# Issuing some of a megakernel's stores and small transfers from ScalarE's DMA queue in place of SyncE's

## The chip, the core and the metric

One core of one Trainium2 chip runs the whole program in one launch. The metric is the device time of an execution in microseconds (us), as the median of several runs. The engines are TensorE (PE, matrix products; PEld its weight loads), VectorE (DVE), ScalarE (ACT, activations and copies), GpSimd (POOL) and SyncE (SP), which in the kernel before only issues DMAs. Each engine runs its own list of instructions in order, and semaphores join the lists.

## The reference

Two layers act on x of 2 x 512 x 512 in float32. Each layer is an attention part and a feed-forward part, and a row of adaptive shifts, scales and gates (from `c` and `wmod`) stands around both.

```python
h = layernorm(x) * (1 + ca) + sa
x = x + ga * L0_attn(h)     # gated linear attention: 32 heads of 128, 8 key heads, chunks of 128
h = layernorm(x) * (1 + cb) + sb
x = x + gb * L0_ffn(h)      # product with a weight of signs, a scale and a bias
...                         # the second layer's own c and wmod
x = x + ga * L1_attn(h)     # softmax attention: 32 heads of 16, 8 key heads, rope, biases
h = layernorm(x) * (1 + cb) + sb
x = x + gb * L1_ffn(h)      # four streams mixed by a 4 x 4 matrix after 50 Sinkhorn iterations
```

What the change touches is the second layer's attention: `softmax(q k^T / 4) v` for each of 32 heads of 16 over 512 tokens, where four query heads share a key and value head.

## The kernel before, in words

**Layer 0** is cut into 64 units of one key head's group of four query heads, one batch and one chunk of 128 tokens. A loop over the units writes the code of each: `scores` (line 523) loads a row of decays `gb` by DMA (L530), masks it on POOL (`dec`, L532), exponentiates it on ACT (L79) and multiplies it with the scores on DVE (L545); `state`, `mix`, `turn` and `project_out` follow. Weights come in by `raw_tile` (L220), are split into a high half on ACT (L229) and a low half on POOL (L232), and each float32 product is made of three products of halves (L254). The halves of an activation are made alike: the high one on ACT (`exact`, L490), the low one on DVE (L491).

**Between the layers**, `tail` (L726) runs beside the later units: the last norms and the feed-forward part of layer 0, and, for each batch, the projections of layer 1. `project_kv` (L717) makes keys and values, `project_q` (L721) one of four tiles of queries. `rope_halves` (L700) takes a projection, adds the bias on ACT (L697), rotates it on DVE and POOL (L704 to L707), copies the result to its high half `hi` on ACT (L709), subtracts that on POOL for the low half `lo` (L711), and stores both in DRAM (L713). `project_kv` stores the values (L719). All these stores are issued from SP's queue.

**Layer 1's attention** has 16 steps (`order`): a batch, a half of the queries and one of four tiles of heads. `queries1` (L849) and `keys1` (L834) load the halves from DRAM into tiles `qs` and `ks`, where the rows of `qs` are high half, low half, high half for each of two head groups, 96 rows in all, and rows 96 to 99 stay free. A step has eight pieces. `maxima_` multiplies queries with keys on PE (L899) and takes each row's maximum over 512 keys on DVE (L903). After every fourth piece the maxima are split into halves (L913 on ACT, L914 on POOL), turned by PE (L917), copied by ACT to a tile `mm` of eight rows and 256 columns (L922), and sent by DMA into rows 96 to 99 of `qs` (L923). There `weigh_` uses them: its product with 100 rows (L937) gives the scores less their maximum, which ACT exponentiates straight out of PSUM (`pt`, L79). `outputs` multiplies the result with the values on PE (`op`, L957) and copies it to `os` on ACT (L971); `finish_` turns it (L980), divides on DVE (L984, L986) and adds it to x on POOL (L992). Ten pieces lie between the maxima of a piece and its weighing (`LAG`).

**Layer 1's streams** follow each half batch: the norm, 50 Sinkhorn iterations on DVE and POOL (L1191 to L1211) and the mix on PE (L1258). The last ones end the program.

**The order of the work.** The code is written in one order of units and pieces, and a scheduler then arranges every engine's list with a model of the instructions' times, priorities (`tc.high_priority`) and added order edges. Such edges are kept in `anchor`: the last instruction of a kind on an engine, behind which the work of `behind()` and `gated()` is kept on the same engine. `scores` sets `anchor["sp"]` to its load of `gb` (L530), and `maxima_` sets it to the transfer of L923. SP's queue holds every DMA of the program, 639 of them, in one order: a DMA whose source or buffer is not ready holds up those behind it. [...]

The DMAs that the change concerns are `k_dram<-hi` and `q_dram<-hi` (L713, 2 and 8 times), `v_dram<-raw` (L719, 2) and `qs<-mm` (L923, 32).

Of the kernel before, what the change touches and what calls it, by code (L numbers as in the profile page):

```python
# [9 lines left out]
FP = mybir.dt.float32  # L10
# [33 lines left out]
H1, KV1, D1 = 32, 8, 16  # L44
# [9 lines left out]
def tile_adaln(ctx: ExitStack, tc: tile.TileContext, a: dict, out: bass.AP):  # L54
    nc = tc.nc
# [82 lines left out]
    anchor = {}  # L138
# [33 lines left out]
    def temp(shape, dt, name, bufs=2):  # L172
        return wk.tile(shape, dt, name=name, bufs=bufs)
# [205 lines left out]
    for kc in range(KC):  # L379
# [13 lines left out]
        out=upto, in_=all1, pattern=[[1, P]], compare_op=ALU.is_ge, fill=0.0, base=0, channel_multiplier=-1,  # L393
# [73 lines left out]
    def project(n, hh, b):  # L467
        hi, lo = W[n, hh]
        ps = bank([P, L], "pps")
        passes(ps, [((hi[:, kc * P:(kc + 1) * P], lo[:, kc * P:(kc + 1) * P]), hcol(b, kc)) for kc in range(KC)])  # L470
        return ps
# [223 lines left out]
    def biased(n, t, i, b):  # L695
        raw = temp([P, L], FP, "raw1")
        nc.scalar.activation(raw, project(n, t, b), AF.Identity, bias=l1c["bias"][:, i:i + 1])  # L697
        return raw

    def rope_halves(n, t, i, b, dst):  # L700

        raw = biased(n, t, i, b)
        rot = temp([P, L], FP, "rot1")
        nc.vector.stream_shuffle(rot, raw, [j ^ 8 for j in range(32)])  # L704
        nc.gpsimd.tensor_tensor(raw, raw, l1c["rope"][0], ALU.mult)
        nc.vector.tensor_tensor(rot, rot, l1c["rope"][1], ALU.mult)
        (nc.gpsimd if RA else nc.vector).tensor_tensor(raw, raw, rot, ALU.add)  # L707
        hi = temp([P, L], FR, "hi1")
        nc.scalar.copy(hi, raw)  # L709
        lo = temp([P, L], FR, "lo1")  # L710
        nc.gpsimd.tensor_tensor(lo, raw, hi.bitcast(FP), ALU.subtract)  # L711
        for src, r in ((hi, 0), (lo, D1)):
            nc.sync.dma_start(out=dst[:, r:r + D1, :], in_=src.bitcast(FP))  # L713

    v_dram = [dram.tile([P, L], FP, name=f"v_dram{b}") for b in range(B)]

    def project_kv(b):  # L717
        rope_halves("wk1", 0, 4, b, k_dram[b])
        nc.sync.dma_start(out=v_dram[b], in_=biased("wv1", 0, 5, b))  # L719

    def project_q(b, t):  # L721
        rope_halves("wq1", t, t, b, q_dram[b][8 * t:8 * t + 8])
# [3 lines left out]
    def tail(n):  # L726
# [4 lines left out]
        for b in range(B):  # L731
# [25 lines left out]
            if c == 8:  # L757
                l1c["there", b] = True
                project_kv(b)
                project_q(b, 0)  # L760
                project_q(b, 1)
            elif c in (10, 12):
                project_q(b, c // 2 - 3)
# [54 lines left out]
    def key_tile(i):  # L818
        return i % 2 if i < TWO else (i - TWO + 2) % 3
# [58 lines left out]
    def maxima(st, k):  # L878
        with urgent(st):
            maxima_(st, k)  # L880
# [9 lines left out]
    def maxima_(st, k):  # L890

        assert holder[key_tile(st["i"])] == st["i"]
        rp, j = divmod(k, 4)
        s, i = divmod(j, 2)
        if j == 0:
            st["m"] = small.tile([P, NQ * 2, 2], FP, name="m")
        for qt in range(NQ):
            ps = psp.tile([P, L], FP, name="s1", bufs=S1)
            anchor["pe"] = nc.tensor.matmul(  # L899
                ps, lhsT=st["qs"][rp][0:KS, i, qt * P:(qt + 1) * P], rhs=st["ks"][s][0:KS],  # L900
                start=True, stop=True,
            ).ins
            anchor["dve"] = nc.vector.tensor_reduce(  # L903
                st["m"][:, 2 * qt + s, i:i + 1], ps, AX.X, ALU.max, negate=True
            ).ins
        if j == 3:
            m2 = small.tile([P, NQ * 2, 2, 2], FR, name="m2")
            hi, lo = m2[:, :, 0], m2[:, :, 1]
            if st is order[-1]:
                nc.vector.tensor_copy(hi, st["m"])  # L910
                nc.vector.tensor_tensor(lo, st["m"], hi.bitcast(FP), ALU.subtract)
            else:
                nc.scalar.copy(hi, st["m"])  # L913
                nc.gpsimd.tensor_tensor(lo, st["m"], hi.bitcast(FP), ALU.subtract)  # L914
            mt = psp.tile([8, Q], FP, name="mt", bufs=MT)
            for qt in range(NQ):
                nc.tensor.transpose(  # L917
                    mt[:, qt * P:(qt + 1) * P],
                    m2[:, 2 * qt:2 * qt + 2].bitcast(FP).rearrange("p a b c -> p (a b c)"), ident,
                )  # L920
            mm = temp([8, L], FR, "mm")[:, 0:Q]
            nc.scalar.copy(mm, mt)  # L922
            anchor["sp"] = nc.sync.dma_start(out=st["qs"][rp].bitcast(FP)[96:100], in_=mm.bitcast(FP)).ins  # L923

    def weigh_(st, k):

# [534 lines left out]
    for n, u in enumerate(units):  # L1461
        g, b, c = u["at"]
# [128 lines left out]
```

## Time and profile before

| | |
|---|---|
| median of 3 runs | 1349.3 us (1343.13 to 1351.8) |
| the profiled execution's own time | 1342.29 us |
| its span, first to last instruction | 1340.5 us |
| granted TensorE clock, mean over the span | 0.969 |
| instructions | 23011 |
| DMA | 109.68 MB, mean 82 GB/s |
| ACT busy, 1060 to 1220 us | 125.18 us of 160 |
| PE busy, 1060 to 1220 us | 156.37 us of 160 |

How to read it: the profile is of one execution. Busy time is the time in which an engine's instruction runs; the issue of a DMA, a wait and a branch do not count as busy, and stand under the engine's sequencer (SPq, ACTq). A matmul's end is modelled, so a busy PE is not a PE at its peak. In a line of the timeline stand start, length, engine, line, operation, output and input, and in brackets the idle time before it with what ended it. In a line of waits stand who waited, at which line, for what, and then the total in us, the times, and the longest. A wait for several semaphores is put down to the one that came last by the profile. In a line of stretches stand the stretch, its length, the busy time of PE, PEld, DVE, ACT and POOL with their instructions, the granted clock, the DMA engines' busy share and GB/s. Times from the span's start say where something lies: layer 0's units fill most of the span, the stores of layer 1's first batch begin at about 818 us, those of the second at about 1049 us, and the last transfer of maxima is issued at 1212.9 us.

### The profile page before, as it was taken

To read this page: it belongs to the slowest core of one execution; us is meant where nothing else is said; L and a number is where in the kernel's file an instruction comes from. 1 tells how busy PE (TensorE), PEld (TensorE's weight loads), DVE (VectorE), ACT (ScalarE), POOL (GpSimd) and SP (SyncE) were. 2 spreads that over 40 slices of the span, in tenths; PEclk is the share of its full clock that TensorE was granted. 3 is DMA by queue.
4 is the path that set the end of the run, shared out by engine and by line. 5 is a ranking of instruction groups with operands and counts; after the bars stand their busy time and mean duration, and the time that the engine had idled before them with its cause. 6 is when DMAs were issued, how large, how long until landed. Compare 5 with 4: busy or idle time off the path is not lost. (4 is left out here: it accounts for less than half of the span.)

```text
span 1340.5 us, 23011 instructions
## 1 busy us (share of the span) xinstructions
PE 1227.8 (92%) x7216; PEld 990.3 (74%) x7216; DVE 1090.6 (81%) x2665; ACT 842.1 (63%) x2375; POOL 790.9 (59%) x1233
## 2 busy tenths in 40 slices
PE   6999999999999999999989999898999999995508
PEld 3787887888788788888877788676777777764408
DVE  7888678777686687877989887877879889898888
ACT  4666665476466466766657675665758678775417
POOL 4446564364265367676788888535435856668751
PEclk9999999999999999999999999998999999998659
DMA  8013331231132143332343233424214221200001
GB/s 258 27 35 110 110 95 40 71 104 55 53 99 85 55 151 94 93 97 95 103 127 110 67 123 89 125 85 129 83 30 124 76 75 50 66 16 2 9 8 48
DMA packets 69762, 109.68 MB, mean 82 GB/s; under 512 B 13436, under 2 KB 20348, under 8 KB 69640
## 3 DMA queue, kind: packets, MB, share of 16 engines
q1 hardware_dynamic: 69640, 108.21, 26.6%
q8 instruction: 57, 0.93, 0.3%
q14 instruction: 65, 0.53, 0.1%
HBM read 99.89 MB, written 8.02 MB: 80 GB/s over the span
## 5 line engine op out<-in xcount | busy, mean ns | idle before, releaser
L903 DVE TENSOR_REDUCE m<-s 128x1 f32<-128x512 f32 x256 | 165.7, 670 | 12.4 <-PE s L899 11.8
L79 ACT ACTIVATE pt<-s 128x512 f32<-128x512 f32 x256 | 137.8, 601 | 12.2 <-PE s L937 11.2
L484 POOL TENSOR_TENSOR q<-xcos,rot 128x512 f32<-128x512 f32 x64 | 95.7, 1495 | 36.6 <-DVE xcos L482 32.9
L79 ACT ACTIVATE sg<-sg 128x512 f32<-128x512 f32 x128 | 80.9, 632 | 55.5 <-DVE sg L515 53.6
L899 PE MATMUL s<-ks,qs 96*128 96x512 f32 x256 | 103.7, 433 | 9.3 <-DVE m L903 7.5
L79 ACT ACTIVATE dec<-dec,room 128x128 f32<-128x128 f32 x256 | 82.9, 398 | 43.2 <-POOL dec L532 43.0
L254 PE MATMUL pps<-hh,wq_h 128*128 128x512 f32 x256 | 102.2, 399 | 0.8 <-DVE zl L608 0.8
L532 POOL TENSOR_SCALAR_AFFINE_SELECT dec<-gb 128x512 f32<-128x512 f32 x64 | 47.0, 734 | 93.3 <-DMA gb<-g_dram 46.0
L254 PE MATMUL ops<-wo_h,zl 128*128 128x512 f32 x256 | 100.9, 394 | 1.0 <-DVE zl L608 0.9
L254 PE MATMUL ops<-wo_h,zh 128*128 128x512 f32 x256 | 101.2, 396 | 0.7 <-DVE zl L608 0.7
L254 PE MATMUL gps<-wg_h,hh 128*128 128x512 f32 x256 | 101.0, 395 | 0.7 <-DVE st L574 0.7
L937 PE MATMUL s<-qs,ks 100*128 100x256 f32 x512 | 98.8, 299 | 1.9 <-ACT pt L79 1.4
L254 PE MATMUL gps<-wg_l,hh 128*128 128x512 f32 x256 | 100.5, 393 | 0.0
L254 PE MATMUL pps<-hl,wq_h 128*128 128x512 f32 x256 | 100.3, 392 | 0.0
L254 PE MATMUL pps<-hh,wq_l 128*128 128x512 f32 x256 | 100.2, 391 | 0.0
L254 PE MATMUL ops<-wo_l,zh 128*128 128x512 f32 x256 | 100.1, 391 | 0.0
L254 PE MATMUL gps<-wg_h,hl 128*128 128x512 f32 x256 | 100.1, 391 | 0.0
L595 DVE SCALAR_TENSOR_TENSOR z<-yps,ss,sg 128x128 f32<-128x128 f32 x256 | 71.8, 340 | 31.1 <-ACT ss L79 30.7
L552 POOL TENSOR_TENSOR gb<-gb,q 128x512 f32<-128x512 f32 x48 | 63.8, 1331 | 55.6 <-ACT gb L79 46.4
L585 PE MATMUL yps<-v,dec 128*128 128x128 f32 x512 | 93.0, 277 | 3.1 <-DVE xcos L482 2.8
L937 PEld LDWEIGHTS s<-qs,ks 100*128 100x128 f32 x512 | 82.2, 193 | 18.2 <-ACT pt L79 5.4
L559 POOL TENSOR_TENSOR xw<-v,room 128x512 f32<-128x512 f32 x48 | 57.2, 1205 | 64.7 <-ACT v L499 61.8
(331 smaller groups left out, 3901.7 us busy)
## 6 DMA issues: line engine op xcount, KB each, us to landing
gb<-g_dram SPq DMA_DIRECT2D x64, 256.0 KB
raw<-in_wq SPq DMA_DIRECT2D x56, 256.0 KB
raw<-in_wg SPq DMA_DIRECT2D x48, 256.0 KB
raw<-in_wo SPq DMA_DIRECT2D x48, 256.0 KB
raw<-in_wmod SPq DMA_DIRECT2D x40, 256.0 KB
qs<-q_dram SPq DMA_DIRECT2D x64, 64.0 KB
raw<-in_wk SPq DMA_DIRECT2D x14, 256.0 KB
raw<-in_wv SPq DMA_DIRECT2D x14, 256.0 KB
```

What stands on the lines that cost most here:

```text
L79: ins = nc.scalar.activation(o, i, func, **kw)
L254: nc.tensor.matmul(ps, lhsT=l, rhs=r, start=i == 0, stop=i == n - 1)
L484: nc.gpsimd.tensor_tensor(dst, sp(xc_), sp(rot), ALU.add)
L532: anchor["pool"] = nc.gpsimd.affine_select(out=dec, in_=gb, pattern=[[0, REP0], [1, P]], compare_op=ALU.is_ge, fill=-1e30, base=0, channel ...
L552: nc.gpsimd.tensor_tensor(gb, gb, q[:, c], ALU.mult)
L559: nc.gpsimd.tensor_tensor(xw, u["v"][:, c, :].unsqueeze(1).to_broadcast(sh4), wdc[:, c, r0:r0 + REP0].unsqueeze(2).to_broadcast(sh4), ALU. ...
L585: nc.tensor.matmul(yps[:, h, :], lhsT=u["pr"][:, h, :], rhs=u["v"][:, c, :], start=True, stop=not c)
L595: nc.vector.scalar_tensor_tensor(z[:, h, :], yps[:, h, :], ss[:, h:h + 1], sg[:, h * P:(h + 1) * P], ALU.mult, ALU.mult)
L899: anchor["pe"] = nc.tensor.matmul(ps, lhsT=st["qs"][rp][0:KS, i, qt * P:(qt + 1) * P], rhs=st["ks"][s][0:KS], start=True, stop=True,).ins
L903: anchor["dve"] = nc.vector.tensor_reduce(st["m"][:, 2 * qt + s, i:i + 1], ps, AX.X, ALU.max, negate=True).ins
L937: nc.tensor.matmul(ps[:, j, :], lhsT=st["ks"][s][0:KM, kt * P:(kt + 1) * P], rhs=st["qs"][rp][0:KM, i, :], start=True, stop=True,)
```

## The change

The high halves' stores, the values' stores and the transfers of the maxima are issued by `nc.scalar` in place of `nc.sync`; the low halves' stores stay on SP. The transfer of the maxima no longer sets `anchor["sp"]`.

```diff
-        for src, r in ((hi, 0), (lo, D1)):
-            nc.sync.dma_start(out=dst[:, r:r + D1, :], in_=src.bitcast(FP))
+        for src, r, queue in ((hi, 0, nc.scalar), (lo, D1, nc.sync)):
+            queue.dma_start(out=dst[:, r:r + D1, :], in_=src.bitcast(FP))
...
-        nc.sync.dma_start(out=v_dram[b], in_=biased("wv1", 0, 5, b))
+        nc.scalar.dma_start(out=v_dram[b], in_=biased("wv1", 0, 5, b))
...
-            anchor["sp"] = nc.sync.dma_start(out=st["qs"][rp].bitcast(FP)[96:100], in_=mm.bitcast(FP)).ins
+            nc.scalar.dma_start(out=st["qs"][rp].bitcast(FP)[96:100], in_=mm.bitcast(FP))
```

44 of SP's 639 DMAs move to ACT's list. As the scheduler works from the whole program, the orders of all five engines differ between the two built programs from that of the first of these stores (818 us in the profile before) on.

## The prediction

> **What bounds the kernel now.** I read the page's busy times and forty slices first, then the busy time by stretch, then the waits of the DMA queue and of ScalarE (ACT), then the order in time around the one long stall.
>
> ```profile
> PE 1227.8 (92%) x7216; PEld 990.3 (74%) x7216; DVE 1090.6 (81%) x2665; ACT 842.1 (63%) x2375; POOL 790.9 (59%) x1233
> PE   6999999999999999999989999898999999995508
> ACT  4666665476466466766657675665758678775417
> ```
>
> After the first slice TensorE (PE) is full nearly everywhere except in the last four, where the layer-1 end runs on VectorE (DVE). Before those, three eights are the only dents, and two of them, slices 26 and 28 (838 to 871 and 905 to 938 us), lie where the change begins. The DMAs that are moved run from 818 us to 1213 us, so I asked for that part by stretch:
>
> ```profile
> 820.00:980.00 160.00, 144.38 (x819) 114.66 (x818) 127.84 (x247) 96.08 (x265) 81.59 (x74) 0.98 0.35 102
> 980.00:1060.00 80.00, 78.49 (x574) 60.51 (x573) 69.19 (x141) 57.56 (x144) 45.94 (x66) 1.00 0.27 80
> 1060.00:1220.00 160.00, 156.37 (x1411) 117.69 (x1410) 142.92 (x465) 125.18 (x312) 102.39 (x397) 0.99 0.19 50
> ```
>
> The columns after the length are PE, PE's weight loads, DVE, ACT, POOL, clock, DMA share, GB/s. PE is idle 15.6 us of the first 160, and hardly at all after that. ACT is idle 64 of 160, 22 of 80, and 35 of 160 us. So something can be won only before 980, and ACT has least room in the last stretch, the attention.
>
> What the SyncE queue (SP) waited for, over the whole span (us in total, times, longest):
>
> ```profile
> SPq L923 <- ACT pt L79: 26.1, 17, 6.8
> SPq L713 <- ACT ss L79: 12.8, 1, 12.8
> SPq L923 <- ACT ss L79: 9.9, 1, 9.9
> ```
>
> Here SP stands in front of a moved store (L713) or a maxima transfer (L923) until ACT has made its source; loads behind it stand too. Around the worst of them, SP's order in time:
>
> ```profile
> 905.71 0.62 SPq L713 DMA_DIRECT2D q_dram<-hi  x1
> ...
> 910.62 0.62 SPq L713 DMA_DIRECT2D q_dram<-lo  x1
> 911.34 0.39 SPq L530 DMA_DIRECT2D gb<-g_dram  x1
> ```
>
> and what that load held up, on POOL, ACT, DVE and PE in turn:
>
> ```profile
> 916.45 0.64 POOL L532 TENSOR_SCALAR_AFFINE_SELECT dec<-gb 128x512 f32<-128x512 f32 x1 [4.17 <-PE ztp L603]
> ```
> ```profile
> 917.12 1.28 ACT L79 ACTIVATE dec<-dec,room 128x128 f32<-128x128 f32 x4 [8.71 <-POOL dec L532]
> ```
> ```profile
> 919.45 3.02 DVE L491 TENSOR_TENSOR ql<-q,qh 128x512 fp32r<-128x512 f32 x2 [5.20 <-ACT qh L490]
> ```
> ```profile
> 923.13 0.79 PE L899 MATMUL s<-ks,qs 96*128 96x512 f32 x1 [5.03 <-DVE m L903]
> ```
>
> The transpose that POOL's line names (ztp) belongs to another tile and reads no gb; what came late was gb, 5.1 us after its issue. PE stood for 5.03 us and then ran slowly, its clock at 0.52 for 7 us:
>
> ```profile
> 923.00:930.00 7.00, 5.94 (x21) 4.70 (x22) 6.79 (x14) 4.47 (x11) 2.72 (x5) 0.52 0.58 168
> ```
>
> **The change part by part.** 44 issues leave SP for ACT's queue: 8 stores of queries' high halves, 2 of keys' and 2 of values, and 32 maxima transfers. The prices are SP's own, as the trace has no DMA on ACT: 0.63 us for a transfer, 0.59 for a query store, 0.63 to 0.70 for a key store, 0.34 for a value store.
>
> ```profile
> L923 SPq DMA_DIRECT2D qs<-mm x32: 625/632/702, 865.9 to 1212.9; - x32
> ```
>
> By stretch, from the same lines within each: up to 980, 6 x 0.668 + 4 x 0.592 + 0.697 + 0.338 = 7.4 us; 980 to 1060, 6 x 0.632 + 0.626 + 0.343 = 4.8 us; 1060 to 1220, 20 x 0.632 + 4 x 0.583 = 15.0 us. Together 27.2 us of ACT's queue.
>
> Part 1, the issue on ACT. At one end it costs nothing, since ACT is idle 121 us of these 400; at the other all 27.2 us are on the path. A gain is excluded: ACT's other instructions stay. In the attention the waits say who is ahead:
>
> ```profile
> ACT os L971 <- PE op L957: 21.1, 19, 1.6
> ...
> ACT pt L79 <- PE s L937: 5.7, 13, 1.3
> ...
> PEld s L937 <- ACT pt L79: 3.1, 11, 0.7
> ```
>
> ACT waits 26.8 us for PE; PE and its weight loads wait 3.7 us for ACT (0.6 of it PE itself). An issue ahead of such a wait only shortens it. In the built order 27 of the 32 transfers stand behind one or more other ACT instructions after their own copy, mostly an exponential of 0.60 us, so the copy is done when the issue comes and the exponential runs beside it. What is queued behind it on ACT is the next exponential, which PE's output product needs, and three score buffers lie between. 3.7 of 30.5 us is 0.12; ACT being fuller then, I take a fifth: 7.4, 4.8 and 15.0 us become 1.5 + 1.0 + 3.0 = 5.5 us.
>
> [...] In the row, SP's q loads in the attention take 303 to 1091 ns to issue, median 424. [...]
>
> Part 2, SP without them. The waits of up to 12.8 us go away where the load behind is late. In the new order SP still has the low half's store ahead of that gb. The high half's copy ended at 905.7; POOL's subtraction, now ahead of two others there, takes 1.28; SP's store 0.62; gb then goes at about 907.7, against 911.3. That is 3.6 us of the 5.03 us stall, and with a stall of 1.4 us I take the slow clock to fall away: 7 us at 0.52 lost 3.4 us. Together -7.0. Late next is that same gb, behind the low half. The ends: 0, if gb's other causes rule, and all of PE's idle time up to 980 with the clock, 15.6 + 3.4 = 19.0 us. I stay nearer the one stall whose cause the rows show.
>
> [...]
>
> Part 3, earlier transfers as such: worth nothing, as no PE score product of L937 waits for a DMA in the trace; LAG keeps ten pieces between a maximum and its use. At the end that cover is gone: the last transfer was issued 0.02 us after its copy (1212.90) and stands in the new order behind two dgx, one copy and two exponentials, some 2 us of work, where the last scores start at about 1217. Ends 0 and 2 us; I take 1.
>
> Part 4, the order. The scheduler rearranged all engines from 818 us on, but the instructions of PE, DVE and POOL are the same in number and kind; 66 of the maxima's and 90 of the scores' products stand ahead of the last layer-0 output product in both, and 501 DVE instructions follow the last attention output in both. The closing 120 us stay. SP's anchor for work of later phases is now a gb load alone, so row tiles load earlier: harmless, DMA is 0.27 busy there.
>
> Sum: 5.5 - 7.0 + 1 = -0.5 us. The profiled execution took 1342.29 (span 1340.5 and 1.8 around it), 7.0 below the median of 1349.3, within the runs' 1343 to 1352; the same difference put on the median gives 1349.
>
> **The rivals.** *Slower: ACT becomes the bound in the attention.* 125.2 + 15.0 = 140.2 of 160 us, in order, with output copies that must wait for PE. For it: DVE is at 142.9 and PE at 156.4, so three engines have little slack and a late exponential shows on PE. Against it: the 26.8 us. Wholly on the path, the issues after 980 cost 19.8; with 1.5 and 1 before and after and the gain of 7.0 that is +15.3, 1364. It decides from 0.72 of the 27.2 us on (27.2 x 0.72 + 1 - 7.0 = 13.6).
>
> [...]
>
> *Faster: SP's freedom removes every dent.* -19.0, and issues at 0.12, +3.3, with no cost at the end: 1334. For it: POOL waited 7.0 us and ACT 2.9 for weight loads in this part too. Against it: the low halves' stores stay.
>
> **How the numbers follow.** Forecast 0.55, ACT bound 0.21, inherited place 0.12, every dent 0.12. About one per cent is what a measurement of this kernel can tell from no change, 13.5 us. The forecast and the inherited place lie within: 0.67; slower 0.21; faster 0.12. The likeliest case's own range is 1339 to 1359 (from no leak with a gain of 10 to half of the issues on the path, 13.6, with a gain of 5 and 1 at the end). For 8 in 10 it reaches to the faster rival and past the slower one: 1334 to 1368.
>
> **What would show it.** Right: ACT carries DMA lines of L713, L719 and L923 of about 0.6 us; SP's waits at them are gone; PE's wait near 918 is under 2 us and the clock near 925 is above 0.9; ACT's wait for op in the attention falls from 21.1 by some 10 us with PE's busy time unchanged. Wrong: PE waits for ACT's exponentials for over 10 us in the attention, issues on ACT over 1 us each, a long ACT wait ahead of the first L923, or a new stall of several us before 980 that the new order made.

## The result, and the profile after

The changed kernel took 1355.1 us in the median of 16 runs (1352.9 to 1358.1), the kernel before 1350.0 (1342.5 to 1352.7) beside it on the same chip: ratio 1.0044, 95% interval 1.0029 to 1.0058, some 5 to 6 us slower. A second comparison gave 1.0046 (1.0031 to 1.0060). That is within one per cent and within the range of the forecast, but it is no tie: my sum said half a microsecond faster, and the intervals are far narrower than the one per cent that the prediction took as the least that a measurement here can tell.

The profiled execution after took 1355.08 us (span 1353.4, mean clock 0.960). The profile of before was of one of its quickest executions (1342.29 of runs up to 1357), so the 12.8 us between the two profiles are more than the change. Where it matters I therefore read x0 below, the same program as before in an execution of 1352.1 us.

The slices of the page after, TensorE and ScalarE:

```profile
PE   6999999999999999999989999898999999995508
ACT  4666665476476466766756676555768678875417
```

The dents of TensorE at 26 and 28 are still there, now at 846 to 880 and 914 to 947 us. The same three stretches as before (columns: stretch, length, busy PE, PEld, DVE, ACT, POOL, clock, DMA share, GB/s):

```profile
820.00:980.00 160.00, 145.68 (x784) 115.79 (x786) 122.71 (x236) 94.04 (x255) 82.06 (x74) 0.93 0.39 116
980.00:1060.00 80.00, 77.93 (x569) 61.19 (x561) 69.39 (x142) 56.11 (x147) 42.53 (x63) 1.00 0.17 51
1060.00:1220.00 160.00, 155.28 (x1357) 114.30 (x1359) 141.06 (x415) 120.88 (x297) 98.33 (x349) 0.98 0.19 52
```

What stands out is the clock of the first stretch: 0.93 in place of 0.98. TensorE is as busy as before there but slower, and its 784 products are 35 fewer. The attention looks much as it did, and its waits say that ACT did not become the bound (total, times, longest, from 1060 to 1220 us):

```profile
ACT os L971 <- PE op L957: 18.2, 17, 1.7
ACT pt L79 <- PE s L937: 7.7, 21, 1.2
PEld s L937 <- ACT pt L79: 4.1, 10, 0.8
...
PE s L937 <- ACT pt L79: 1.3, 3, 0.6
```

At the scores' product (L937), TensorE and its weight loads wait 5.4 us for the exponentials where it was 3.7, and ACT still waits 25.9 us for TensorE. The 32 transfers cost on ACT what they cost on SP (median 0.637 us, where it was 0.632):

```profile
L923 ACTq DMA_DIRECT2D qs<-mm x32: 636/637/713, 876.4 to 1225.2; - x32
```

### The profile page after: what moved, and what is told of

It is laid out like the page before. It is cut to its first block, busy times and chain, and to the rows that moved or that the text cites. A ratio compares the mean times of both kernels' runs of the same rounds, so it can differ in the third digit from the quotient of the medians.

```text
span 1353.4 us, 22997 instructions
## 1 busy us (share of the span) xinstructions
PE 1239.1 (92%) x7216; PEld 997.5 (74%) x7216; DVE 1092.6 (81%) x2665; ACT 844.2 (62%) x2375; POOL 788.9 (58%) x1233
## 5 line engine op out<-in xcount | busy, mean ns | idle before, releaser
L79 ACT ACTIVATE pt<-s 128x512 f32<-128x512 f32 x256 | 139.1, 600 | 21.1 <-PE s L937 12.9
L937 PE MATMUL s<-qs,ks 100*128 100x256 f32 x512 | 100.4, 300 | 2.7 <-ACT pt L79 1.3
L937 PEld LDWEIGHTS s<-qs,ks 100*128 100x128 f32 x512 | 82.3, 193 | 19.4 <-ACT pt L79 5.6
L595 DVE SCALAR_TENSOR_TENSOR z<-yps,ss,sg 128x128 f32<-128x128 f32 x256 | 71.7, 341 | 27.0 <-ACT ss L79 26.5
```

Source lines behind the costliest of these rows:

```text
L79: ins = nc.scalar.activation(o, i, func, **kw)
L595: nc.vector.scalar_tensor_tensor(z[:, h, :], yps[:, h, :], ss[:, h:h + 1], sg[:, h * P:(h + 1) * P], ALU.mult, ALU.mult)
L937: nc.tensor.matmul(ps[:, j, :], lhsT=st["ks"][s][0:KM, kt * P:(kt + 1) * P], rhs=st["qs"][rp][0:KM, i, :], start=True, stop=True,)
```

## The experiments

**How an order is pinned.** The three edited lines change two things: which queue issues 44 DMAs, and, through the scheduler, the order of every engine's list. Theory *order* says that the new lists cost the time, which part 4 of the prediction took as nothing. Theory *issue* says that ACT's 27 us of issue do, part 1. (The expectations below say "step" for a part.) To part them, a list of instruction names per engine, taken from a built program, is replayed at the end of the program's code by order edges. The instructions have the same names in both kernels:

```diff
+    traced = {i.name: i for i in nc.cur_bb.bb.instructions}
+    for names in replayed():
+        for before_, then in zip(names, names[1:]):
+            tc.add_manual_dep(traced[then], before_, order_only, reason="a replayed order")
```

Every kernel below has this but x3 and the changed kernel measured again. Ratios below are to the kernel before, run beside it on the same chip, with the 95% interval.

**x0: the order of before, replayed, nothing else.** 

> The kernel before, with its own order on every engine pinned by order edges instead of found by the scheduler: a control, so that the pinning can be used in the other kernels. Both theories expect the time of the kernel before, ratio 1.000 +- 0.002, and the same profile within 2 us at every product. A difference of more than 3 us would mean that pinning itself costs or moves something, and that x1 and x2 must be read against this kernel and not against before.


Measured 1.0000 (0.9982 to 1.0017). Pinning costs nothing that shows.

**x1: the changed order without the change.** The edits of the change are taken back (all DMAs on `nc.sync`), and the changed kernel's lists replayed. 

> All 639 DMAs stay on SP, and the order of the instructions of every engine (and of the DMAs among them) is that of the changed kernel: the new order without the issue on ACT. Theory order (the loss comes from the rearranged lists, step 4 of the prediction, which I took as nothing): about +5 us against before (+3 to +9), with the delay at the products of L899 by 880 us of about 10 us again. Theory issue (the loss is ACT's 27.2 us of issue on the path, step 1): 0 or less, -2 to +1. Against both: SP has the waits in front of L713 and L923 again, which could cost several us of its own; then POOL's dec waits for gb show it.


Measured 1.0055 (1.0034 to 1.0076): +7.4 us. The order alone makes a loss at least as large as the change's; the two intervals overlap.

**x2: the change without the changed order.** The edits of the change, and the lists of before with each moved issue one ACT instruction behind its copy. 

> The 44 DMAs are issued from ACT, and every other instruction of PE, DVE, POOL and ACT stands in the order of the kernel before; each moved issue stands one ACT instruction behind the copy that makes its source. This is the issue on ACT and the freed SP without the new order. Theory order: no slower than before, -4 to +1 us, as SP's waits at L713 and L923 are gone and ACT's issues lie in its idle time; the stall of PE near 918 us shrinks. Theory issue: about +5 us (+3 to +8), most of it gathered between 1060 and 1220 us, with more PE waits for ACT's pt than before's 3.7 us.


Measured 1.0012 (0.9995 to 1.0029). In the middle that is +1.6 us, where theory issue wanted 3 us or more. Its interval ends at +3.9 us, so the issues can hold a part of the loss at most. But the gain that part 2 promised is not there either.

**x3: the anchor alone.** One word of the change:

```diff
-            anchor["sp"] = nc.sync.dma_start(out=st["qs"][rp].bitcast(FP)[96:100], in_=mm.bitcast(FP)).ins
+            nc.sync.dma_start(out=st["qs"][rp].bitcast(FP)[96:100], in_=mm.bitcast(FP))
```

> Only one word of the change: the transfer of the maxima stays on SP but no longer sets the anchor for SP, so the scheduler is free to make another order, and no DMA changes its queue. Theory order: it differs from before by several us in either direction (2 to 8), since a new list for every engine is what costs. Theory issue: 0, within 2 us.


Measured 1.0028 (1.0011 to 1.0044), +3.8 us, with every DMA in its old queue. I had called this edge harmless.

**x8: the suspected cost almost doubled.** As x2, and each transfer of the maxima in two halves:

```diff
-            nc.scalar.dma_start(out=st["qs"][rp].bitcast(FP)[96:100], in_=mm.bitcast(FP))
+            for a in (0, 2): nc.scalar.dma_start(out=st["qs"][rp].bitcast(FP)[96 + a:98 + a], in_=mm.bitcast(FP)[2 * a:2 * a + 4])
```

> As x2, and each of the 32 transfers of the maxima is issued on ACT as two of half the rows, one right behind the other: 32 x 0.63 = 20 us more of ACT's queue, from 27 to 47 us, with nothing else moved. Theory issue (ACT's time is on the path at a fifth or more): +4 us or more against x2, ratio to before 1.004 or more. Theory order (issues lie in ACT's idle time): 0 to +1.5 us against x2, ratio 1.000 to 1.0025.


Measured 1.0021 (1.0005 to 1.0038), 0.0009 above x2: 1.2 us for 20 us more of ACT's queue, 6% on the path. The two intervals overlap, and together they allow anything from nothing to about a fifth. Another reading is x1 against the changed kernel, the same lists with the issues on SP and on ACT: 1.0055 and 1.0044, so the issues on ACT show no cost there either. By the middle of these intervals, ACT's issues lie mostly in its idle time.

**Where the order loses: equal work.** The lists differ, so the same instruction is no mark to compare by. Instead each product of TensorE was weighed by the median duration of its kind, and the time read at which each kernel had done the same amount of work. The table gives what a kernel lost against x0 while doing the work that x0 does in three stretches, worked out from the profiled traces (one execution each; before has the lists of x0, and its row shows 1 to 3.5 us of scatter: from 820 to 980 us TensorE was idle 15.6 us in before and 15.5 in x0, at a mean clock of 0.98 and 0.95):

| kernel | order up to 905 us, behind it | 830 to 900 | 900 to 960 | 960 to 1220 | ratio |
|---|---|---|---|---|---|
| before | before, before | -1.1 | -1.2 | -3.5 | |
| x2 | before, before | +0.8 | -1.1 | -0.3 | 1.0012 |
| x8 | before, before | -1.7 | -0.7 | +0.8 | 1.0021 |
| after | after, after | +5.2 | -2.4 | +2.5 | 1.0044 |
| after, again | after, after | +6.1 | -1.9 | +2.5 | 1.0046 |
| x1 | after, after | +9.2 | -1.3 | +0.7 | 1.0055 |
| x3 | its own | -0.5 | -0.8 | +5.6 | 1.0028 |

The changed order loses 5 to 9 us between 830 and 900 us, before the attention has the machine for itself. x3's order loses elsewhere, and why was not traced further. What the loss consists of can be estimated from the stretch from 830 to 900 us, here in x0, in x2, after, and after again:

```profile
830.00:900.00 70.00, 62.10 (x294) 49.49 (x294) 55.72 (x106) 38.34 (x110) 39.78 (x34) 0.98 0.43 118
830.00:900.00 70.00, 64.79 (x290) 51.53 (x289) 56.01 (x107) 38.67 (x101) 36.76 (x32) 0.93 0.42 118
830.00:900.00 70.00, 61.10 (x270) 48.08 (x269) 51.99 (x97) 34.42 (x99) 34.56 (x30) 0.90 0.37 110
830.00:900.00 70.00, 58.82 (x266) 46.38 (x265) 50.57 (x97) 34.50 (x100) 33.25 (x29) 0.93 0.37 110
```

Take TensorE's idle time, and 70 us times the part of the clock that was not granted: 7.9 + 1.4 us in x0, 5.2 + 4.9 in x2, 8.9 + 7.0 after and 11.2 + 4.9 after again. Against x0 the sums are +0.8, +6.6 and +6.8 us, near the table's +0.8, +5.2 and +6.1. So idle time and slow clock make the loss together, in shares that differ between two executions of the same kernel. A slow clock does not suffice: x2 has one, with less idle time, and loses 0.8.

Two kernels put the place of the loss to the test: the lists of one order up to the 29th product of the maxima (about 905 us), those of the other from there, and ACT issues in both.

**h1: before up to 905 us, then after.** 

> The 44 issues on ACT throughout; every engine's list is that of before up to the 29th product of the maxima (about 905 us) and from there in the changed kernel's order. If the loss lies in the changed order between 840 and 905 us, as the comparison of equal work says (+6 to +9 us between 860 and 890): the time of x2, ratio 0.999 to 1.002. If it is spread over the attention, or lies behind 905: 1.003 to 1.006.


Measured 0.9992 (0.9979 to 1.0004), with -0.3 us in the first stretch. Everything behind 905 us in the changed order, the attention included and with the issues on ACT, costs nothing on the whole.

**h2: after up to 905 us, then before.** 

> The counterpart: the changed kernel's order up to the 29th product of the maxima, then the order of before, all 44 issues on ACT. If the loss lies between 840 and 905 us: the whole of it stays, ratio 1.003 to 1.006. If it lies behind 905: 0.999 to 1.002.


Measured 1.0035 (1.0022 to 1.0048), with +6.3 us in the first stretch. The loss is there. Busy times and clock from 850 to 890 us, in x0, in h1, after, and in h2:

```profile
850.00:890.00 40.00, 35.87 (x173) 27.73 (x172) 34.39 (x66) 21.95 (x61) 21.55 (x20) 1.00 0.39 105
```
```profile
850.00:890.00 40.00, 37.34 (x171) 29.20 (x170) 34.09 (x69) 23.70 (x66) 22.00 (x20) 0.96 0.36 93
```
```profile
850.00:890.00 40.00, 33.46 (x143) 25.34 (x142) 34.73 (x70) 20.85 (x61) 19.98 (x18) 0.87 0.35 103
```
```profile
850.00:890.00 40.00, 32.19 (x130) 22.86 (x130) 33.32 (x70) 20.84 (x61) 20.32 (x19) 0.87 0.34 102
```

With the changed lists TensorE does 130 to 143 products in these 40 us instead of 171 to 173: it is idle 2.4 to 3.7 us more than in x0, and its clock is 0.87.

**x4: one wait in that stretch.** The first long idle time there, in the profile after, on DVE and then on PE:

```profile
863.51 1.74 DVE L491 TENSOR_TENSOR ql<-q,qh 128x512 fp32r<-128x512 f32 x1 [1.56 <-POOL w_l L232]
865.17 0.85 DVE L545 SCALAR_TENSOR_TENSOR dec<-sps,room,dec 128x128 f32<-128x128 f32 x3
```
```profile
866.18 0.77 PE L254 MATMUL ops<-wo_h,zh 128*128 128x512 f32 x1 [3.43 <-DVE dec L545]
```

The first line names POOL's w_l for ql's wait, but the built program has no wait of ql for w_l. It waits for POOL's `lo`, done at 860.78, and for the landing of the store of `hi`, issued on ACT at 859.43. The scratch tiles of layer 0 and layer 1 share one pool, and in the changed order ql was given the buffer that `hi` left: in that program the two have one address. x1, where the same store is on SP, shows such a wait by name: ACT's qh stood 2.9 us for the DMA q_dram<-hi. Behind ql on DVE stood three of the unit's four dec products, and behind those TensorE. x4 replays the changed kernel's order with ql moved behind them and behind the unit's zl. 

> The changed kernel with its own order pinned, and one VectorE instruction moved: the low half ql of a later unit's queries (L491), which took over the buffer of a high half hi and so waited for that store to land, now stands behind the three remaining dec products (L545) of the unit at hand and behind its zl (L608). Theory order, in the sharp form that this one place makes the loss: the 3.4 us stall of TensorE at about 866 us falls to under 2 us, the slow clock behind it goes, and the time is 3 to 7 us under the changed kernel's, so 1348 to 1352 where before has 1350, ratio 0.999 to 1.002. Theory issue, or order as a loss spread over many places: within 1.5 us of the changed kernel, ratio 1.003 to 1.006.


Measured 1.0029 (1.0015 to 1.0043); the stall is 1.8 us now, in another product:

```profile
866.35 0.50 PE L254 MATMUL ops<-wo_h,zl 128*128 128x512 f32 x1 [1.76 <-DVE zl L608]
```

The first stretch costs +3.8 in place of 5.2 and 6.1. So this wait seems worth some 2 us, by the stretch and by the ratios (1.0029 against 1.0044 and 1.0046, with intervals that overlap), and is not the whole.

**x9: the crowd behind it.** The second idle time after, in steps of 3 us:

```profile
878.00:881.00 3.00, 1.89 (x11) 1.22 (x9) 3.00 (x9) 3.00 (x13) 2.63 (x3) 1.00 0.23 75
881.00:884.00 3.00, 2.22 (x9) 1.22 (x8) 3.00 (x7) 2.09 (x7) 0.20 (x1) 0.85 0.27 100
884.00:887.00 3.00, 2.09 (x7) 1.44 (x6) 2.96 (x8) 0.36 (x1) 0.00 (x0) 0.50 0.00 0
887.00:890.00 3.00, 3.00 (x10) 2.43 (x10) 1.03 (x2) 1.19 (x2) 0.00 (x0) 0.51 0.01 3
```

DVE is full from 878 to 887, TensorE idles 2.8 of these 9 us in gaps of 0.6 to 1.1 us, mostly ahead of products of the maxima, and from 884 to 890 it gets half its clock. x9 is x4 with two of these products put among the twelve of pps that follow, and with sg and z (L518, L595) put ahead of some reductions on DVE. 

> The changed kernel's order with ql moved as in x4, and the second half of the suspected loss taken apart: in x4 VectorE is busy without a gap from 874 to 887 us while TensorE, which has mostly maxima products there, is busy 6.9 of the 9 us from 878 and gets a clock of 0.5 to 0.6 from 884 to 890. Here two maxima products are put among the 12 products of pps that follow, and VectorE's sg and z (L518, L595) in front of the reductions that crowd there. If this bunch is the rest of the loss: TensorE's idle time from 878 to 887 falls by 1 us or more, the slow clock goes, and the time is 2 to 4 us under x4's 1.0029, ratio 0.999 to 1.0015. If the rest of the loss is elsewhere between 840 and 905: 1.002 to 1.004, as x4.


Measured 1.0026 (1.0009 to 1.0043), as x4. But TensorE's idle time from 878 to 887 fell only from x4's 2.1 to 1.8 us and the slow clock came all the same (0.57, 0.50 and 0.79 in the steps of 3 us from 881), so the suspected cause was not taken away: this run decides nothing.

**h3 and h4: the cut at 870 us.** The same crossing as h1 and h2, cut at one entry of TensorE's list at about 870 us. 

> All 44 issues on ACT; the order of before up to the 3785th product of TensorE (about 870 us), the changed kernel's order from there. It keeps what the changed order does after 870 (maxima crowded on VectorE, slow clock) and drops the wait for the high half's store before it. If the loss is mostly the wait before 870: 0.999 to 1.001. If mostly the stretch behind 870: 1.003 to 1.005. If it is shared: 1.001 to 1.003.

> The counterpart: the changed kernel's order up to the 3785th product of TensorE, the order of before from there, all 44 issues on ACT. If the loss is mostly the wait before 870: 1.003 to 1.005. If mostly behind 870: 0.999 to 1.001. If it is shared: 1.001 to 1.003. h3 and h4 together should add up to h1 and the changed kernel's 1.0046.


Measured 1.0060 (1.0040 to 1.0081) and 1.0047 (1.0027 to 1.0067). They don't add up: h3, without the wait, loses 7.3 us in the first stretch, at a new seam of its own (TensorE busy 5.3 of the 10 us from 880, clock 0.60). The lists of this stretch hang together, and how much of the idle time and of the slow clock is due to the wait and how much to the crowd stays open.

**x6 and x5: what the late load is worth.** x2 left open why the gain of part 2 did not come. In x2, SP's waits from 895 to 930 us, and its order:

```profile
SPq L849 <- DMA q_dram<-hi: 15.6, 1, 15.6
```
```profile
911.84 0.79 SPq L849 DMA_DIRECT2D qs<-q_dram  x2
912.68 0.58 SPq L713 DMA_DIRECT2D q_dram<-lo  x1
913.38 0.38 SPq L530 DMA_DIRECT2D gb<-g_dram  x1
```

The store of `hi` left SP and ACT issued it at 907.84, right behind its copy. The next two DMAs in SP's list load queries from what that store writes, and wait for it to land; gb is behind them. It goes 5.5 us after the store is issued; before, it was 5.6 us (905.71 to 911.34). The wait of 12.8 us for the copy and the 3.3 us for the landing became one of 15.6 us. In before's list, these two loads are the line that I left out of the fence in the prediction, between 905.71 and 910.62:

```profile
909.78 0.80 SPq L849 DMA_DIRECT2D qs<-q_dram  x2
```

x6 is the kernel before with its order pinned and gb moved ahead of the high half's store on SP; x5 is x2 with gb ahead of those two loads. As `gated()` holds gb behind the work beside it on its own engine, the edge is left out for SP, where the pinned list stands in for it:

```diff
-            if e != "free" and m.name not in past:
+            if e not in ("free", "sp") and m.name not in past:
```

> The kernel before with its own order and no issue on ACT; only the same load of gb is put in front of the high half's store on SP. If the gain that step 2 forecast needs the load's place alone and no other queue: the same -5 to -8 us, ratio 0.994 to 0.997. If it needs the stores off SP: 0.

> As x2 (order of before, 44 issues on ACT), and on SP one load of gb (L530) is put in front of the two loads of q_dram (L849) that wait for the high half's store to land. If step 2's stall is the load's place on SP, as x2's wait of 15.6 us says, the 5 us stall of TensorE near 922 us and the slow clock behind it go: -5 to -8 us against x2, ratio to before 0.994 to 0.998. If another input of the unit is late just behind gb: 0 to -2 against x2.


Measured 0.9969 (0.9957 to 0.9981) for x6 and 0.9973 (0.9955 to 0.9991) for x5: -4.2 us for x6, and for x5 -5.3 against x2 by their two ratios. gb leaves at 900.69 in x6, and TensorE's longest wait there is

```profile
923.30 0.73 PE L899 MATMUL s<-ks,qs 96*128 96x512 f32 x2 [0.86 <-DVE m L903]
```

where it was 5.03. The slow clock behind the stall did not go with it, though. In x6, before and behind 924 us:

```profile
920.60:924.00 3.40, 2.19 (x12) 1.35 (x10) 3.40 (x5) 3.35 (x8) 3.40 (x4) 1.00 0.81 235
924.00:930.80 6.80, 6.45 (x27) 5.55 (x26) 6.80 (x15) 2.66 (x6) 3.46 (x5) 0.50 0.60 188
```

One load's place in SP's list is worth 4 to 5 of the 7 us that I hoped for from the change, and needs no other queue.

**x7 and b1: the same in the changed order.** x7 is x4 with gb ahead of the low half's store, b1 is h1 with the same move. 

> The changed kernel's order with ql moved as in x4, and on SP the load of gb put in front of the low half's store that waits 10.8 us for POOL. The stall of 3.6 us near 929 us goes as in x5 and x6, -4 to -6 against x4's 1.0029: ratio 0.998 to 1.000. If the new order has another input late just behind gb: 1.002 to 1.004.

> The best of what was seen: the order of before up to 905 us, the changed kernel's order from there, the 44 issues on ACT, and the load of gb in front of the low half's store that waits. Both theories expect the sum of h1 and of the load's place: 0.9992 less 0.003 to 0.005, ratio 0.994 to 0.997. If gb's place is worth less in this order (x7 kept 2.6 of its 3.9 us of stall): 0.997 to 0.999.


Measured 1.0014 (1.0003 to 1.0025) and 0.9990 (0.9972 to 1.0008). TensorE's stall near 925 us falls to 2.6 and 2.7 us only; what else is late there in this order was not traced. The parts do not add, and the best kernel of the study is x6, which has nothing of the change in it.

**The changed kernel again.** 

> The changed kernel as it is, beside the others on the same chip: ratio 1.003 to 1.006 by every theory; x4, x7, h1 and h2 are read against it.


Measured 1.0046 (1.0031 to 1.0060).

## Why the prediction was wrong, by its steps

**Part 1, the issue on ACT: too dear.** The price of one was right (0.637 us on ACT, 0.632 on SP; 0.59 for a query store and 0.34 for a value store, as on SP). The 5.5 us did not show: x8 has 0.06 in place of a fifth for 20 us more (with room up to about a fifth), and x2, which has all 27 us and the freed SP, is at +1.6 us (-0.7 to +3.9). The rows that I read (ACT waits 26.8 us for TensorE, TensorE 3.7 for ACT) said so; the fifth was a guess on top of them. Those 3.7 us also left out 1.5 us of the output product's weight loads (L957), which went to 0.7. The rival of ACT as the bound wanted 10 us of PE's waits; it got 1.3. One sign of being right was missed here: ACT's wait for op fell from 21.1 to 18.2 us, not by some 10.

**Part 2, SP without the waits: a gain that never came.** This part failed: the change doesn't bring gb forward. Its price was too high as well. An earlier gb is worth 4.2 us in x6 and 5.3 in x5, not 7.0; in x6's profile the stall went from 5.03 to 0.86 us, but the 3.4 us of clock, which I had only assumed to go with the stall, did not follow (0.57 from 923 to 930 us, 0.52 before), while x5's has 0.97 there. The view had the answer: the waits of SP list "L849 <- DMA q_dram<-hi", and the two loads stand between the store and gb. In the changed order the queue has another head again: the copy of `hi` comes at 913.07, and the low half's store waits 10.8 us for POOL. SP after, then POOL and PE:

```profile
915.09 0.58 SPq L713 DMA_DIRECT2D q_dram<-lo  x1
915.77 0.42 SPq L530 DMA_DIRECT2D gb<-g_dram  x1
```
```profile
920.85 0.63 POOL L532 TENSOR_SCALAR_AFFINE_SELECT dec<-gb 128x512 f32<-128x512 f32 x1 [3.78 <-DMA gb<-g_dram]
```
```profile
929.11 0.79 PE L899 MATMUL s<-ks,qs 96*128 96x512 f32 x1 [3.63 <-DVE m L903]
```

Of the 5.03 us, 1.4 went, and the slow clock behind the stall stayed (0.50 for the next 7 us). The prediction's mark, under 2 us and a clock above 0.9, was missed.

With this part at nothing, as x2 suggests, my sum would have been 1356 (1349.3 + 5.5 + 1). That this meets the measured 1355 is luck: it gets there by the 5.5 us of part 1, which the runs do not show, and without the order, which they do.

**Part 3, the transfers: right, and the 1 us at the end was nothing.** Behind the work that x0 does up to 1220 us, the changed kernel loses -0.3 and -0.1 us in its two profiles.

**Part 4, the order: taken as nothing, and it is the result.** This is the part that set the sign. I compared counts of instructions and the place of three kinds of them, found them alike, and priced the rearrangement at zero and the dropped anchor as harmless. Measured, the order is worth +5.2 and +6.1 us between 830 and 900 us, +7.4 us in x1 without any issue on ACT, and the anchor alone +3.8 in x3. The prediction's last sentence named "a new stall of several us before 980 that the new order made" as what would prove it wrong; it came at 866 us. The order had no term in the sum and no chance among the rivals, where a bound of some us to either side belonged.

The chance of 0.12 for an inherited place, and its share of the 0.67, stand on a wait of ACT that no run shows. Ahead of the first L923, where the prediction's last sentence has a long one, there was none: it was issued at 876.43, 0.03 us after its copy ended, and the waits of ACT's queue at the 32 transfers took 0.038 us at most each.

## What to carry to other kernels

Before a DMA is moved to free a queue, read what stands behind it in the old queue: if the next entry reads what the moved one writes, the wait only changes its name (in x2, 12.8 and 3.3 us became one of 15.6). Where a scheduler makes the lists, a three-line edit is a new program; pin the old order to measure the edit and the new order to measure the scheduler, and until then give the order a price with two signs. Here the late load was cheaper to move within its own queue than its neighbours were to another one. Both new orders of the scheduler, the changed kernel's and x3's, lost; whether before's is an unusually good one, two orders cannot tell.

## What the runs showed of the hardware that was not expected

The kernel before takes 1342 to 1357 us from one execution to the next, with the same instructions. Over the 124 of its runs beside the experiments, the time follows the mean granted clock (correlation -0.81): at 0.967 to 0.969 the runs took 1343 to 1345 us, at 0.957 they have a median of 1352.4. Much the same stall is answered differently from one execution to another: near 840 us, ahead of the same product, TensorE waited 2.52 us in the profile of before and kept a clock of 1.00 from 838 to 846 us; in x2 it waited 2.65 us and got 0.79. Nor did a long wait stand ahead of every slow clock: in x6 it was 0.50 for 6.8 us behind 3.4 us in which TensorE was idle 1.2 us in all and never longer than 0.86. So the slow clock near 925 us, which before and after show behind stalls of 5.03 and 3.63 us, came in x6 without a long stall. What sets it, no row shows.

A transfer of half the size took nearly as long to issue on ACT: 0.619 us for 4 KB in x8, 0.637 for 8 KB in the changed kernel. Of the ACT issues only the store of the first batch's keys took longer, 1.17 to 1.19 us in x2, x8 and after, where the second batch's takes 0.63; what held it up, no row shows.
